# A selective-scan layer: one quarter of B's product on GpSimd, one activation table for exp and ln, and another order for the first chunk

## The chip, the cores and the metric

The kernel runs on one core of a Trainium2 chip. A core has five engines that work in parallel, each with its own queue of instructions in order: TensorE (PE, matrix products into PSUM), VectorE (DVE), ScalarE (ACT, activation functions), GpSimd (POOL) and SyncE (SP, which here issues the transfers). Engines wait for each other through semaphores. The metric is the device time of one execution in microseconds (us), the median of several runs.

## The reference

Four images of 256 channels and 64 x 64 positions pass through four residual layers, each `x = x + layer(groupnorm(x))`. Layers 0 to 2 (a deformable convolution, an attention and a deformable aggregation) are not touched. Layer 3 is a Mamba block over the 4096 positions taken as a sequence:

```
xz = xs @ in_proj_w.T;  u, res = split(xz)            # 512 channels each
u = silu(causal_conv4(u) + conv_b)
dt, Bm, Cm = split(u @ x_proj_w.T)                    # 16, 16, 16
delta = softplus(dt @ dt_proj_w.T + dt_proj_b)
state = exp(delta * A) * state + delta * Bm * u       # 512 x 16 states, per position
y = sum over n of state * Cm  +  u * D
out = (y * silu(res)) @ out_proj_w.T
```

## The kernel before

Images are worked one after the other. For each, layer 3 (`layer3`) cuts the sequence into 8 chunks of 512 positions, and keeps the 512 channels as 4 groups of 128 partitions. A **step** is one state n of one chunk: 8 chunks x 16 states, 128 steps for an image. In a step

- TensorE spreads row n of B over the partitions, as a product of a 0/1 matrix with `bp` into the PSUM tile `bn` (L1419; `bn` has one buffer, so the next row waits until the product has read this one);
- VectorE multiplies `h = du * bn` (L1491, 128 x 2048), du being delta times u;
- ScalarE makes `da = exp(delta * A)` for each group of channels (L1498, two PSUM buffers);
- VectorE runs the recurrence as four scans (L1499);
- GpSimd keeps the last column (`carry`, L1510) and multiplies `h` by row n of C, `cn` (L1513). `cn` is fetched by SP from a small DRAM tensor `cd`, spread over 128 partitions (L1417, six buffers);
- TensorE adds h to `y` through an identity matrix (L1411), two steps behind (`add`).

Beside the steps of chunk j runs the preparation of chunk j+1 (`front`), cut into small parts that are hung into numbered half steps: normalise (`xn`, L1245), project (L1213), convolve (L1259, a product with diagonal matrices), silu (L1273), the product for dt, B and C (L1282, `dbc`), softplus as Abs, Relu, exp and ln (L1303 to L1330), the gates (L1213 again) and a split of B into three bf16 terms (`split`, L1342 to L1350). Seen from the running chunk, these parts begin in step 12 with xn, the convolutions fall in steps 14, 15, 0 and 1, silu in step 2, `dbc` in step 3, and ln in step 9; for the first chunk they come two steps later. The output of chunk j-1 is projected in steps 7 and 9 of chunk j (`close`, L1369). Statistics of the next image (L152) run on VectorE in between.

The order on TensorE, ScalarE, VectorE and GpSimd is the order in which the code emits the instructions (`tc.manual_schedule`). SP's order is left to the planner.

`first()` prepares chunk 0 before any step. It projects and convolves by turns on TensorE, copies on VectorE, applies silu, makes `dbc`, and computes softplus with the differences on VectorE. What of chunk 1's preparation would fall before step 0 (normalising on GpSimd and three projections through one PSUM bank) follows it from the list `begin`. ScalarE has to load a table before a function that the loaded one lacks; the kernel has such loads at silu, at exp and at ln.

Of the kernel before, what the change touches and what calls it, by code (L numbers as in the profile page):

```python
# [9 lines left out]
F32 = mybir.dt.float32  # L10
I32 = mybir.dt.int32
BF16 = mybir.dt.bfloat16
AF = mybir.ActivationFunctionType
# [3 lines left out]
P = 128  # L17
# [46 lines left out]
class Net:  # L64
# [1016 lines left out]
    def layer3(self, x, out, nxt, early):  # L1081
# [4 lines left out]

        nc, tc = self.nc, self.tc
        C = 512
        NC, LEAD = N // C, 4
        with (  # L1090
# [29 lines left out]
            tiny = pa.tile([P, 1], F32, tag="tiny", name="tiny")  # L1120
# [4 lines left out]

            def first():


                c = chunks[0]
                spare = lambda: py.tile([P, C], F32, tag="y", name="front")  # L1130
                xn = pa.tile([P, 2, C], F32, tag="xn3", name="xn3")
# [12 lines left out]
                def project(dc):  # L1144
                    pu = spare()
                    for ct in range(2):
                        nc.tensor.matmul(pu, win[:, ct, bass.ts(dc, P)], xn[:, ct, :], start=(ct == 0), stop=(ct == 1))
                    nc.vector.tensor_copy(up[:, dc, 3:], pu)

                def convolve(dc):  # L1150
                    cv = spare()
                    for i in range(4):
                        nc.tensor.matmul(cv, conv[:, dc, i, :], up[:, dc, i : i + C], start=(i == 0), stop=(i == 3))
                    nc.scalar.activation(u[:, dc, :], cv, AF.Silu, bias=cb[:, dc : dc + 1])

                project(0)
                project(1)
                convolve(0)
                project(2)
                convolve(1)  # L1160
                project(3)
                nc.gpsimd.tensor_copy(tail, up[:, :, C : C + 3])
                convolve(2)
                convolve(3)
                px = bank()
                for dc in range(4):
                    nc.tensor.matmul(px, xpw[:, dc, :], u[:, dc, :], start=(dc == 0), stop=(dc == 3))
                nc.scalar.activation(tiny, self.eps, AF.Exp)
                dbc = pa.tile([P, C], F32, tag="dbc", name="dbc")
                nc.scalar.copy(dbc, px)  # L1170
                c["cd"] = self.dram.tile([DS, C], F32, tag="cd", name="cd")
                nc.sync.dma_start(out=c["cd"], in_=dbc[16:32, :])
# [4 lines left out]

                c["gates"] = [spare() for _ in range(4)]
                for dc, pg in enumerate(c["gates"]):
                    for ct in range(2):  # L1180
                        nc.tensor.matmul(
                            pg, win[:, ct, bass.ts(4 + dc, P)], xn[:, ct, :], start=(ct == 0), stop=(ct == 1)
                        )
# [4 lines left out]
                for lo, hi in ((0, 64), (64, 96), (96, 128)):  # L1188
                    nc.gpsimd.tensor_copy(bp[lo:hi], dbc[lo:hi])
                    if hi < P:  # L1190
                        nc.gpsimd.tensor_copy(t[hi:], dbc[hi:])
                        nc.gpsimd.tensor_sub(dbc[hi:], dbc[hi:], t[hi:])
                for dc in range(4):
                    nc.scalar.activation(w[:, dc, :], pzs[dc], AF.Abs, bias=dtb[:, dc : dc + 1])
                    nc.scalar.activation(du[:, dc, :], w[:, dc, :], AF.Exp, scale=-1.0)
                    nc.vector.tensor_scalar(delta[:, dc, :], pzs[dc], dtb[:, dc : dc + 1], 0.0, ALU.add, ALU.max)
                    nc.vector.tensor_scalar_add(w[:, dc, :], du[:, dc, :], 1.0)
                    nc.vector.scalar_tensor_tensor(
                        du[:, dc, :], w[:, dc, :], -1.0, du[:, dc, :], ALU.add, ALU.subtract
                    )  # L1200
                    nc.vector.tensor_sub(delta[:, dc, :], delta[:, dc, :], du[:, dc, :])
                for dc in range(4):
                    nc.scalar.activation(w[:, dc, :], w[:, dc, :], AF.Ln)
                    nc.vector.tensor_add(delta[:, dc, :], delta[:, dc, :], w[:, dc, :])
                    nc.vector.tensor_mul(du[:, dc, :], delta[:, dc, :], u[:, dc, :])
# [25 lines left out]
            def front(j):  # L1231
# [6 lines left out]
                def begin():  # L1238
                    xn = c["xn"] = pa.tile([P, 2, C], F32, tag="xn3", name="xn3")
                    for ct in range(2):  # L1240
                        to, xs, m, a = xn[:, ct, :], x[:, ct, bass.ts(j, C)], rs[:, ct : ct + 1], shift[:, ct : ct + 1]
                        if j == 1:
                            nc.gpsimd.tensor_scalar(to, xs, m, a, ALU.mult, ALU.add)
                        else:
                            nc.scalar.activation(to, xs, AF.Identity, bias=a, scale=m)  # L1245
                    c["up"] = pa.tile([P, 4, C + 3], F32, tag="up", name="up")
                    nc.gpsimd.tensor_copy(c["up"][:, :, 0:3], tail)
                    c["u"] = pb.tile([P, 4, C], F32, tag="u", name="u")
# [23 lines left out]
                def silu():  # L1272
                    nc.scalar.activation(c["u"], c["u"], AF.Silu)  # L1273
                    gate_silu(j - 1)

# [8 lines left out]
                def keep():  # L1284
                    c["dbc"] = pa.tile([P, C], F32, tag="dbc", name="dbc")
                    nc.scalar.copy(c["dbc"], c["b"])

                    c["cd"] = self.dram.tile([DS, C], F32, tag="cd", name="cd")
                    nc.sync.dma_start(out=c["cd"], in_=c["dbc"][16:32, :])
# [123 lines left out]
            def state(j, n):  # L1413

                c = chunks[j]
                cn = c["cn", n] = pb.tile([P, 1, C], F32, tag="cn", name="cn", bufs=6)
                nc.sync.dma_start(out=cn, in_=c["cd"][n : n + 1, :].unsqueeze(0).to_broadcast([P, 1, C]))  # L1417
                bn = c["bn", n] = pbb.tile([P, 1, C], F32, tag="bn", name="bn")
                nc.tensor.matmul(bn[:, 0, :], pick[:, n, :], c["bp"], start=True, stop=True)  # L1419
# [3 lines left out]
            begin = []  # L1423
            for j in range(1, NC):
                for step, half, pe, rest in front(j):
                    at = DS * (j - 1) - (LEAD if j > 1 else 2) + step
                    if at < 0:
                        begin.append((pe, rest))
                    else:
                        slots.setdefault((at, half), []).append((pe, rest))  # L1430
# [5 lines left out]
            slots.setdefault((last + 2, 0), []).append((None, lambda: gate_silu(NC - 1)))  # L1436
# [33 lines left out]
            with tc.manual_schedule(  # L1470
# [8 lines left out]
                for pe, rest in begin:  # L1479
                    if pe:  # L1480
                        pe()
                    rest()
                state(0, 0)
# [3 lines left out]
                for s in range(total):  # L1487
                    j, n = s // DS, s % DS
                    c = chunks[j]
                    h = pb.tile([P, 4, C], F32, tag="h", name="h", bufs=4)  # L1490
                    nc.vector.tensor_mul(h, c["du"], c.pop(("bn", n)).to_broadcast([P, 4, C]))  # L1491
# [12 lines left out]
                    scan(1)  # L1504
                    empty(s, 0)
# [12 lines left out]
                    if s + 1 < total:  # L1518
                        state((s + 1) // DS, (s + 1) % DS)
# [134 lines left out]
```

## Time and profile before

| what | us |
|---|---|
| median of 3 runs (lowest, highest) | 9984.5 (9975.76, 9988.26) |
| the profiled execution, its own time | 9981.35 |
| its span, first to last instruction | 9979.5 |
| first image: layers 0 to 2 up to layer 3's first norm | 1516.5 |
| first image: preparation, to the first product of step 0 | 55.2 |
| first image: 128 steps | 959 |
| busy of the span: PE, DVE, ACT, POOL | 8624.9, 7632.5, 4959.9, 6758.0 |

The four images repeat the same pattern; their first products of layer 3 (L1491) start at 1571.7, 4045.1, 6517.5 and 8993.3 us. The granted TensorE clock is 0.956 on average.

A row of the timeline reads: start in us, duration in us, engine, line of the kernel, operation, tile written <- tiles read, shapes, count; in brackets, how long the engine was idle before it and which instruction ended that. A row of the page's costliest groups reads: line, engine, operation, tiles, shapes, count | busy us, mean ns of one | idle us before them, and what ended most of it. A matrix product in f32 shows as two passes, each with a MATMUL of its own.

### The profile page before, as it was taken

To read this page: it belongs to the slowest core of one execution; us is meant where nothing else is said; L and a number is where in the kernel's file an instruction comes from. 1 tells how busy PE (TensorE), PEld (TensorE's weight loads), DVE (VectorE), ACT (ScalarE), POOL (GpSimd) and SP (SyncE) were. 2 spreads that over 40 slices of the span, in tenths; PEclk is the share of its full clock that TensorE was granted. 3 is DMA by queue.
4 is the path that set the end of the run, shared out by engine and by line. 5 is a ranking of instruction groups with operands and counts; after the bars stand their busy time and mean duration, and the time that the engine had idled before them with its cause. 6 is when DMAs were issued, how large, how long until landed. Compare 5 with 4: busy or idle time off the path is not lost. (4 is left out here: it accounts for less than half of the span.)

```text
span 9979.5 us, 88756 instructions
## 1 busy us (share of the span) xinstructions
PE 8624.9 (86%) x29193; PEld 4231.9 (42%) x29193; DVE 7632.5 (76%) x8183; ACT 4959.9 (50%) x7576; POOL 6758.0 (68%) x3948
## 2 busy tenths in 40 slices
PE   5889998998778999899877899989977789998997
PEld 3643443333464344333346434433335643443333
DVE  4764597999676459899967646889996764679998
ACT  3743335665474332566557433266645733326664
POOL 3746786887574667688747467768875746777876
PEclk9999999999899999999989999999998999999999
DMA  7830011111793011111188201111118810111111
GB/s 264 319 138 1 31 48 38 46 45 49 258 329 113 1 34 52 36 46 45 44 293 324 82 1 40 48 40 44 45 42 313 322 63 1 42 52 34 40 41 33
DMA packets 377891, 956.56 MB, mean 96 GB/s; under 512 B 34675, under 2 KB 107820, under 8 KB 375372
## 3 DMA queue, kind: packets, MB, share of 16 engines
q0 software_dynamic: 165888, 604.05, 16.8%
q1 hardware_dynamic: 211532, 346.73, 11.1%
q8 instruction: 234, 3.83, 0.2%
q14 instruction: 237, 1.94, 0.1%
HBM read 784.59 MB, written 92.32 MB: 88 GB/s over the span
## 5 line engine op out<-in xcount | busy, mean ns | idle before, releaser
L1499 DVE TENSOR_TENSOR_SCAN h<-da,carry,h 128x512 f32<-128x512 f32 x2048 | 2470.5, 1264 | 138.3 <-ACT da L1498 89.7
L1513 POOL TENSOR_TENSOR h<-h,cn 128x2048 f32<-128x2048 f32 x508 | 2300.1, 4528 | 41.0 <-POOL carry L1510 0.2
L1498 ACT ACTIVATE da<-delta,l3a 128x512 f32<-128x512 f32 x2048 | 1389.1, 689 | 1138.6 <-DVE h L1499 1136.4
L1411 PE MATMUL y<-h,ident 128*128 128x512 f32 x4096 | 1930.8, 616 | 3.3 <-POOL h L1513 2.5
L344 POOL DMA_INDIRECT g<-tab,idx x1152 | 1355.1, 1176 | 756.7 <-issue 368.8
L565 POOL TENSOR_TENSOR acc<-acc,e 128x1024 f32<-128x1024 f32 x480 | 1125.2, 2344 | 541.6 <-ACT e L561 520.1
L388 PE MATMUL pz<-cols,l0w 128*128 128x256 f32 x4608 | 1216.2, 411 | 191.5 <-DVE cols L377 81.3
L1411 PEld LDWEIGHTS y<-h,ident 128*128 128x128 f32 x4096 | 809.8, 198 | 1295.1 <-issue 1233.3
L1491 DVE TENSOR_TENSOR h<-du,bn 128x2048 f32<-128x2048 f32 x512 | 1157.8, 2261 | 34.4 <-PE bn L1419 34.3
L353 DVE SCALAR_TENSOR_TENSOR r<-g,wx,r 128x512 f32<-128x512 f32 x1152 | 858.1, 745 | 368.2 <-ACT r L352 252.2
L462 DVE TENSOR_REDUCE m<-pm 128x3 f32<-128x1536 f32 (+2 forms) x340 | 599.3, 1763 | 699.7 <-PE pm L452 699.7
L388 PEld LDWEIGHTS pz<-cols,l0w 128*128 128x128 f32 x4608 | 896.4, 205 | 361.2 <-DVE cols L377 119.1
L561 ACT ACTIVATE e<-sc 128x1024 f32<-128x1024 f32 x512 | 496.0, 1020 | 1029.7 <-PE sc L548 1029.7
L572 PE MATMUL cx<-e,v 128*128 128x512 f32 x2048 | 1001.1, 616 | 0.0
L845 DVE TENSOR_TENSOR prod<-ring,A 128x1280 f32<-128x1280 f32 x640 | 922.6, 1480 | 79.1 <-DMA ring<-ring 60.8
L352 ACT ACTIVATE r<-g,wx 128x512 f32<-128x512 f32 x1152 | 826.4, 717 | 258.9 <-DMA g<-tab,idx 212.9
L862 PE MATMUL pacc<-prod,ident 128*128 128x512 f32 x1920 | 912.9, 609 | 35.3 <-DVE prod L845 23.3
L854 POOL TENSOR_TENSOR prod<-prod 128x512 f32<-128x512 f32 x640 | 800.1, 1274 | 184.2 <-DVE prod L845 161.6
L370 PE MATMUL pt<-ident,acc 128*128 128x128 f32 x2304 | 426.7, 294 | 297.2 <-DVE acc L361 232.9
L1510 POOL COPY carry<-h 128x4 f32<-128x4 f32 x512 | 98.0, 191 | 804.6 <-DVE h L1499 793.0
L572 PEld LDWEIGHTS cx<-e,v 128*128 128x128 f32 x2048 | 352.4, 189 | 599.1 <-issue 596.6
L360 ACT ACTIVATE acc<-r,wy 128x256 f32<-128x256 f32 x1152 | 571.9, 496 | 24.6 <-DVE r L353 22.1
(254 smaller groups left out, 10959.9 us busy)
## 6 DMA issues: line engine op xcount, KB each, us to landing
cn<-cd SPq DMA_DIRECT2D x512, 256.0 KB
tab<-vt SPq DMA_DIRECT2D x112, 640.0 KB
ring<-ring SPq DMA_DIRECT2D x288, 126.0 KB
ring<-ring SPq DMA_DIRECT2D x288, 124.0 KB
g<-tab,idx POOLq DMA_INDIRECT x1152
x<-in_x SPq DMA_DIRECT2D x64, 256.0 KB
out<-x SPq DMA_DIRECT2D x56, 256.0 KB
l0w<-in_l0w SPq DMA_DIRECT2D x4, 2304.0 KB
```

Source lines behind the costliest of these rows:

```text
L344: nc.gpsimd.indirect_dma_start(out=g[:], out_offset=None, in_=tab[:, :], in_offset=bass.IndirectOffsetOnAxis(ap=idx[:, t, k : k + 1], axis=0),
L353: nc.vector.scalar_tensor_tensor(r, g[:, :, 1, :], wx[:, 1, t, k : k + 1], r, ALU.mult, ALU.add)
L388: nc.tensor.matmul(sums[m][:, ot, :256], wf[:, i, bass.ts(ot, P)], cols[m][:, i, :], start=(i == 0), stop=(i == 17),)
L565: nc.gpsimd.tensor_add(b["acc"], b["acc"], e)
L572: nc.tensor.matmul(blocks[qb]["cx"], v[:, 4 * (i + kt // 4 * 4) + kt % 4, :], e[:, bass.ts(i % 2, 512)], start=(kt == 0 and i == 0), stop= ...
L845: nc.vector.tensor_mul(d["prod"][:, :, t, :].rearrange("p x (g c) -> p x g c", c=GC), ring[y // VR % 4][:, :, y % VR, :].rearrange("p x (g ...
L862: nc.tensor.matmul(d["pd"], self.ident, prod[:, wx, :], start=(wy == 0 and wx == 4), stop=(wy == WIN - 1 and wx == 2),)
L1411: nc.tensor.matmul(c["ys"][dc], self.ident, h[:, dc, :], start=False, stop=(n == DS - 1))
L1491: nc.vector.tensor_mul(h, c["du"], c.pop(("bn", n)).to_broadcast([P, 4, C]))
L1498: nc.scalar.activation(da, c["delta"][:, dc, :], AF.Exp, scale=al[:, dc, n : n + 1])
L1499: nc.vector.tensor_tensor_scan(h[:, dc, :], da, h[:, dc, :], carry[:, dc, n : n + 1], ALU.mult, ALU.add)
L1513: nc.gpsimd.tensor_mul(h, h, cn.to_broadcast([P, 4, C]))
```

## The change

It has four parts, all in `layer3`.

1. In the eight steps n = 14, 15, 0, 1, 2, 3, 4, 5 of each chunk VectorE's product covers three of the four channel groups, and GpSimd multiplies the fourth (`quarter`). GpSimd does not read `bn`: for these steps row n of B comes like `cn` from DRAM. `cd` now holds the rows of C and B, and SP fetches `bs` with two buffers; `cn` has four. Both are issued two steps ahead (`ahead`). `quarter(s + 1)` stands in GpSimd's queue in the middle of step s, ahead of its carry copy and product with cn.
2. After each silu the table set with both exp and ln is loaded by name (`tables`).
3. `first()` is ordered anew. All four projections come first; groups 0 and 2 are copied by ScalarE and convolved on TensorE, groups 1 and 3 are copied and convolved by VectorE (one product and three multiply-adds). In softplus, ScalarE makes Relu and GpSimd the subtraction, the split of B lies between those, and ln of a group follows exp of the next.
4. Chunk 1's normalising moves forward on GpSimd, and its three projections go into three PSUM banks, ahead of chunk 0's gates. The list `begin` is gone.

```diff
-                for dc in range(4):
-                    nc.tensor.matmul(px, xpw[:, dc, :], u[:, dc, :], start=(dc == 0), stop=(dc == 3))
-                nc.scalar.activation(tiny, self.eps, AF.Exp)
+                for dc in range(4):
                     pu = spare()
...
+                    project(pu, xn, dc)
+                    if dc % 2:
+                        nc.vector.tensor_copy(up[:, dc, 3:], pu)
+                        nc.vector.tensor_scalar_mul(u[:, dc, :], up[:, dc, :C], cw[:, dc, 0:1])
+                        for i in range(1, 4):
+                            nc.vector.scalar_tensor_tensor(
+                                u[:, dc, :], up[:, dc, i : i + C], cw[:, dc, i : i + 1], u[:, dc, :], ALU.mult, ALU.add
+                            )
+                    else:
+                        nc.scalar.copy(up[:, dc, 3:], pu)
...
+                    nc.gpsimd.tensor_scalar(
+                        c1["xn"][:, ct, :], x[:, ct, C : 2 * C], rs[:, ct : ct + 1], shift[:, ct : ct + 1], ALU.mult, ALU.add
+                    )
...
+                for dc in (0, 2):
                     cv = spare()
                     for i in range(4):
                         nc.tensor.matmul(cv, conv[:, dc, i, :], up[:, dc, i : i + C], start=(i == 0), stop=(i == 3))
+                    nc.scalar.activation(u[:, dc + 1, :], u[:, dc + 1, :], AF.Silu, bias=cb[:, dc + 1 : dc + 2])
                     nc.scalar.activation(u[:, dc, :], cv, AF.Silu, bias=cb[:, dc : dc + 1])
...
+                for k, dc in enumerate((1, 3, 0, 2)):
+                    nc.tensor.matmul(px, xpw[:, dc, :], u[:, dc, :], start=(k == 0), stop=(k == 3))
+                tables()
...
+                pus = []
+                for dc in range(3):
+                    pus.append(pda.tile([P, C], F32, tag="da", name="front") if dc else bank())
+                    project(pus[dc], c1["xn"], dc)
...
                 for dc in range(4):
                     nc.scalar.activation(w[:, dc, :], pzs[dc], AF.Abs, bias=dtb[:, dc : dc + 1])
                     nc.scalar.activation(du[:, dc, :], w[:, dc, :], AF.Exp, scale=-1.0)
-                    nc.vector.tensor_scalar(delta[:, dc, :], pzs[dc], dtb[:, dc : dc + 1], 0.0, ALU.add, ALU.max)
+                    nc.scalar.activation(delta[:, dc, :], pzs[dc], AF.Relu, bias=dtb[:, dc : dc + 1])
...
-                    nc.vector.tensor_sub(delta[:, dc, :], delta[:, dc, :], du[:, dc, :])
+                    nc.gpsimd.tensor_sub(delta[:, dc, :], delta[:, dc, :], du[:, dc, :])
+                    if dc < 3:
+                        split(*((0, 64), (64, 96), (96, 128))[dc])
+                    if dc:
+                        end(dc - 1)
+                end(3)
+                for dc in range(3):
+                    nc.scalar.copy(c1["up"][:, dc, 3:], pus[dc])
...
                     nc.scalar.activation(c["u"], c["u"], AF.Silu)
                     gate_silu(j - 1)
+                    tables()
...
+            hs, helped = {}, (14, 15, 0, 1, 2, 3, 4, 5)
+
+            def ahead(s):
+
+                if s < NC * DS:
+                    j, n = s // DS, s % DS
+                    c = chunks[j]
+                    for name, r, bufs in (("cn", n, 4), ("bs", DS + n, 2)):
+                        if name == "cn" or n in helped:
+                            t = c[name, n] = pb.tile([P, 1, C], F32, tag=name, name=name, bufs=bufs)
+                            nc.sync.dma_start(
+                                out=t, in_=c["cd"][r : r + 1, :].unsqueeze(0).to_broadcast([P, 1, C])
+                            )
...
+            def quarter(s):
+
+                if s < NC * DS:
+                    c = chunks[s // DS]
+                    hs[s] = pb.tile([P, 4, C], F32, tag="h", name="h", bufs=4)
+                    if s % DS in helped:
+                        nc.gpsimd.tensor_mul(hs[s][:, 3:4, :], c["du"][:, 3:4, :], c.pop(("bs", s % DS)))
...
-                    h = pb.tile([P, 4, C], F32, tag="h", name="h", bufs=4)
-                    nc.vector.tensor_mul(h, c["du"], c.pop(("bn", n)).to_broadcast([P, 4, C]))
+                    h = hs.pop(s)
+                    d = 3 if n in helped else 4
+                    nc.vector.tensor_mul(
+                        h[:, :d, :], c["du"][:, :d, :], c.pop(("bn", n)).to_broadcast([P, d, C])
+                    )
+                    ahead(s + 2)
...
                     scan(0)
                     scan(1)
+                    quarter(s + 1)
                     empty(s, 0)
```

## The prediction

> **What bounds the kernel now.** I began with the page: VectorE is 76% busy over the span, GpSimd 68%, TensorE 86%, so no single engine explains it. The windows by stage then put the change's reach at four stretches of about 1016 us (layer 3 of each image): a preparation of 55.2 us, from 1516.5 to 1571.7 in the first image, in which VectorE is busy for 21 us and TensorE for 47.8, and 128 steps in which VectorE is busy over 96% of the time. The costliest rows of the page are those steps:
>
> ```profile
> L1499 DVE TENSOR_TENSOR_SCAN h<-da,carry,h 128x512 f32<-128x512 f32 x2048 | 2470.5, 1264 | 138.3 <-ACT da L1498 89.7
> L1513 POOL TENSOR_TENSOR h<-h,cn 128x2048 f32<-128x2048 f32 x508 | 2300.1, 4528 | 41.0 <-POOL carry L1510 0.2
> L1491 DVE TENSOR_TENSOR h<-du,bn 128x2048 f32<-128x2048 f32 x512 | 1157.8, 2261 | 34.4 <-PE bn L1419 34.3
> ```
>
> A plain step is 2.26 us of L1491 and four scans, 7.09 us from one L1491 to the next. That says "VectorE". The timeline says which steps that is true of. Here are VectorE's products from step 14 of one chunk to step 3 of the next:
>
> ```profile
> 2158.25 2.26 DVE L1491 TENSOR_TENSOR h<-du,bn 128x2048 f32<-128x2048 f32 x1
> ...
> 2165.81 2.29 DVE L1491 TENSOR_TENSOR h<-du,bn 128x2048 f32<-128x2048 f32 x1 [0.39 <-PE bn L1419]
> ...
> 2172.93 2.26 DVE L1491 TENSOR_TENSOR h<-du,bn 128x2048 f32<-128x2048 f32 x1
> ...
> 2195.72 2.46 DVE L1499 TENSOR_TENSOR_SCAN h<-da,carry,h 128x512 f32<-128x512 f32 x2 [1.60 <-ACT da L1498]
> 2198.09 2.26 DVE L1491 TENSOR_TENSOR h<-du,bn 128x2048 f32<-128x2048 f32 x1
> ```
>
> and TensorE in the same stretch:
>
> ```profile
> 2165.32 0.38 PE L1419 MATMUL bn<-bp,pickn 128*128 128x512 bf16 x1
> 2165.54 3.60 PE L1411 MATMUL y<-h,ident 128*128 128x512 f32 x8
> 2168.97 3.60 PE L1259 MATMUL front<-up,conv 128*128 128x512 f32 x8
> 2172.41 0.38 PE L1419 MATMUL bn<-bp,pickn 128*128 128x512 bf16 x1
> ```
>
> TensorE has no gap: 8 passes for y, 8 for the next chunk's convolution, one for bn, 2172.41 - 2165.32 = 7.09 us. VectorE's product waits for that bn. **Steps 15, 0 and 1 are TensorE's**, and happen to cost what VectorE costs. Step 2 (10.99 us) is ScalarE's: it starts from the last convolution and ends at the exp that the scan waited 1.60 us for:
>
> ```profile
> 2186.78 0.69 ACT L1264 ACTIVATE u<-front,l3b 128x512 f32<-128x512 f32 x1 [1.22 <-PE front L1259]
> ...
> 2188.67 1.28 ACT L1273 ACT_TABLE_LOAD   x1
> 2189.97 1.91 ACT L1273 ACTIVATE u<-u 128x2048 f32<-128x2048 f32 x1
> 2191.78 1.89 ACT L1229 ACTIVATE sres<-sres 128x2048 f32<-128x2048 f32 x1
> 2193.69 1.28 ACT L1498 ACT_TABLE_LOAD   x1
> ```
>
> Before that, TensorE's row at 2145.73 (first projection, fed by xn in step 12) starts a chain without slack to 2165.32. So steps 12 to 2 are a fixed 54.0 us; only steps 3 to 11 are free to follow VectorE.
>
> **Part 1: GpSimd takes a quarter of the product in steps 14, 15, 0 to 5.** Eight products of 16 shrink from 2048 to 1536 elements. Slope between two VectorE rows: (2.259 - 1.225)/1024 = 1.01 ns per element (L1491 and L1515), so 512 elements are 0.52 us; a step becomes 6.57. Counted everywhere that is 256 x 0.52 = 133 us. By the rows above it pays only where VectorE sets the step:
> - Chunks 1 to 5: steps 3, 4, 5: 1.56 us. In 14, 15, 0, 1 it becomes a wait for bn; in 2 a wait for exp.
> - Chunk 6 (no next front in its steps 14 and 15): 5 x 0.52 = 2.6.
> - Chunk 7 (no front at all): 8 x 0.52 = 4.2.
> - Chunk 0: steps 1, 2, 3, 5 give 2.1; step 0 falls from 7.57 to 6.57 (its table load and late copies go), 1.0; step 4 (10.5 us) is the silu chain, nothing.
>
> The cost falls on GpSimd. Its nearest rows are L1513 over four, 1.13 us, and L854 at 1.27; the worst is L1192, 1.65 beside VectorE. I take 1.2. Its period in a helped step is 4.53 + 0.19 + 1.2 + some 0.3 between = 6.2 us, under 6.57, and it lies ahead of the carry copy and h x cn in GpSimd's queue, which TensorE's sum takes up two steps later, so over 5 us of cover. The tight place is step 15, where `du` of the next chunk (L1330, 4.53 us) stands ahead: quarter 15 ends at 2170.0 by the middle-chunk rows, scan 3 wants it at 2171.1; in chunk 0 it is late by 0.3 us, which I charge. The added row fetches (256 of 256 KB) are like L1417's and are issued two steps, some 13 us, ahead on SP's queue, behind cn of the same step; cn's buffers fall from 6 to 4, still two steps of cover. I charge nothing; without that cover, each late row would stall GpSimd's carry and h x cn. Floor 0, ceiling about 1 us per chunk.
>
> The Trainium skill speaks against such a transfer: "SBUF — State Buffer", "Who interferes with whom", says that a VectorE instruction with two SBUF inputs contends with a GpSimd instruction that reads SBUF. The row that shows it is L1516, 3.38 us for half of an h that takes 2.26 by L1513's rate, beside L1515. In the steps VectorE's second operand (bn, da) lies in PSUM and L1513 stays at 4.51 to 4.57, so I use 1.2; with 1.12 more for every quarter GpSimd would reach 7.3 us in a helped step.
>
> **Part 2: one table for exp and ln.** In the loop this removes Ln's load and exp's reload, 2 x 1.28 us per chunk in ScalarE's queue, at step 9 (11 in chunk 0). In the last image, where nothing else hides it:
>
> ```profile
> 9424.10 1.28 ACT L1326 ACT_TABLE_LOAD   x1
> 9425.39 1.91 ACT L1326 ACTIVATE w<-w 128x2048 f32<-128x2048 f32 x1
> 9427.32 1.28 ACT L1498 ACT_TABLE_LOAD   x1
> ```
>
> Without both, the next exp is ready before the scan needs it, so the whole stall goes: 2.05 us in chunk 0, 1.36 in chunks 1 to 6 of the last image, but 0.36 in the others, where two statistics of the next image (L152, 1.0 us) fill VectorE meanwhile. Half of these 0.36 I drop, since TensorE reaches step 12 no earlier where its sums in step 8 ran slowly (5.29 us for 8 passes against 3.60). The skill ("ScalarE: Activation LUTs", "What ACT_TABLE_LOAD costs") gives 2.66 us for a switch, a drain included; here the instruction after the load starts 1.29 us after it began. By the page the pair would be 5.3 us, but the gain would be the same: it is capped by the wait that VectorE has.
>
> Sum of the loop: chunk 0: 2.1 + 1.0 + 2.05 - 0.3 = 4.9; chunks 1 to 5: 5 x (1.56 + 0.2) = 8.8 (last image 5 x 2.92 = 14.6); chunk 6: 2.9 (4.0); chunk 7: 4.2. That is 20.8 for three images, 27.7 for the last: **90 us**.
>
> **Part 3: the first chunk's preparation.** Today it ends with a chain through one PSUM bank: project, copy, project, and then bn:
>
> ```profile
> 1562.60 0.58 ACT L1217 COPY up<-front 128x512 f32<-128x512 f32 x1 [4.92 <-PE front L1213]
> 1567.06 0.59 ACT L1217 COPY up<-front 128x512 f32<-128x512 f32 x1 [3.87 <-PE front L1213]
> 1571.48 0.59 ACT L1217 COPY up<-front 128x512 f32<-128x512 f32 x1 [3.83 <-PE front L1213]
> ```
>
> The new order, from TensorE's start at 1517.2. Four projections: 5.1 us for the first two as now, 8 passes x 0.43 = 3.4 for the others, to 1525.8. Two convolutions on TensorE, 16 passes, 6.9, to 1532.7. VectorE's two (copy 0.69, product 0.42 to 0.73, three accumulations of 0.69 to 0.98 each) end near 1527 and 1531, beside them. The product with xpw: 3.4, of which the last quarter waits for silu (0.69): 1536.2, where it now is 1543.8. dbc copy 0.58, then 1.2 to the first Abs: 1538.1. ScalarE: Abs, exp and now Relu, 0.7 + 0.54 + 0.57 = 1.8 us per part, plus Ln 0.63; VectorE's first difference is out at 1540.9. From there GpSimd's queue is the longest: four subtractions (1.16 to 1.65 each; L1344 and L1192) and the split of dbc, whose seven rows take 6.7 today: 10.1 to 12.3 us, to 1551.0 to 1553.2. Then one add and one product on VectorE, 1.4: 1552.4 to 1554.6, against 1571.7. ScalarE ends by 1549.7, gates by 1548.3, bn follows the split. Chunk 1's normalisation (L1243, 2.50 us) moves to GpSimd's idle stretch before dbc, its three projections (5.2 us of TensorE) to between the dtw products and the gates while ScalarE works, their copies (1.7 us) behind the last Ln; uncovered they would cost these times. The cd write doubles to 64 KB on SP, 10 us and more before its first use by quarter 0. I take 1553.5: 18.2, say **18 us per image, 72 in all**. Were each GpSimd instruction to wait out a VectorE one (the port rule read as a full block), the subtractions are 1.86 each and the start 1 to 2 us later.
>
> **Sum.** 90 + 72 = 162 us. The profiled execution took 9981.35 us, its span 9979.5; the median shown is 9984.5, 3 us above, so I subtract there: **9822 us**.
>
> **Rivals.**
> - *VectorE stays the bound in all steps* (TensorE moves up with it). 133 + 23 of table stalls + 2 + 72 = 230: 9754. For it: VectorE at 96%. Against: the gapless TensorE rows. 12%.
> - *The preparation gains half*: GpSimd's alternating queue and the two waits on it per part stretch to about 1561. 90 + 40: 9854. 16%.
> - *The loads stay* or come back at each change between exp and Ln. In the preparation these alternate: 7 x 1.28 = 9 us per image, and the loop loses its 22: 162 - 36 - 22 = 104: 9880. 6%.
> - *Slower: GpSimd becomes the bound.* Per chunk it has 16 x 5.0 + 4 x 4.53 + 2.5 for the splits = 100.6, plus 8 quarters of 1.2 = 110 of 117.6 us. A quarter of 2.15 us fills it; from 2.8 us, 5.1 more per chunk, the 162 are used up. At 3.2, each with the 1.12 of L1516 and a late row, about 126 per chunk: 32 x 8.4 = 270 lost against the forecast: 10090. For it: GpSimd runs 2 us behind at step 13 already. Against: bn and da in PSUM. 6%.
>
> The forecast itself 58%; 2% for no change. A measurement of this kernel can tell about 0.2%, 20 us. Faster 0.92, same 0.02, slower 0.06. The range takes in the second rival, most of the way to the first, and the unknown costs: 9764 to 9868.
>
> **What would show it.** L1491's successor: 256 products of 128x1536 near 1.74 us; GpSimd quarters near 1.2. Steps 3, 4, 5 at 6.57; steps 15, 0, 1 still at 7.09, with more idle on VectorE released by bn; step 2 still near 11. No load at Ln. First product about 36 us after the first projection instead of 54.5. It is wrong if steps 14 to 1 shorten, if scans wait for GpSimd, or if TensorE's rows in steps 12 to 15 close up.

## The result

| | before | after |
|---|---|---|
| median of 4 runs (lowest, highest), us | 9980.13 (9975.66, 9988.26) | 9836.97 (9825.3, 9840.41) |
| the profiled execution, us | 9981.35 | 9825.3 |
| its span, us | 9979.5 | 9823.5 |
| granted TensorE clock, mean | 0.956 | 0.959 |

The ratio is 0.9855, with an interval of 0.9841 to 0.9869: 143 us faster by the medians. The forecast was 9822.

The two traces, cut at the same instructions, say where it came from. "128 steps" runs from the first product of step 0 to the product of the last step; "preparation" from the last L176 of the norm (its line in both kernels) to that first product. Each figure is a sum over four images.

| stretch, us | before | after | gain | forecast |
|---|---|---|---|---|
| 128 steps | 3803.0 | 3711.7 | 91.3 | 90 |
| preparation | 214.0 | 164.2 | 49.8 | 72 |
| the rest: layers 0 to 2, both ends | 5962.5 | 5947.6 | 14.9 | 0 |

The last row is not the change's: its code is the same in both, and the profiled execution of after was the fastest of its four. The change is worth 141 us by these two traces, with the steps where the forecast had them and the preparation 22 us short.

The costliest rows of after that answer to those of before (the page's groups):

```profile
L1548 DVE TENSOR_TENSOR_SCAN h<-da,carry,h 128x512 f32<-128x512 f32 x2048 | 2469.0, 1264 | 138.3 <-ACT da L1547 78.0
L1563 POOL TENSOR_TENSOR h<-h,cn 128x2048 f32<-128x2048 f32 x508 | 2299.7, 4527 | 41.3 <-POOL carry L1560 0.8
...
L1537 DVE TENSOR_TENSOR h<-du,bn 128x2048 f32<-128x2048 f32 (+1 forms) x512 | 1022.8, 1998 | 49.9 <-PE bn L1460 49.8
```

Scans and GpSimd's products with cn cost what they did. B's product lost 1157.8 - 1022.8 = 135 us of VectorE's work, the 133 of the prediction's first reckoning. Only half of that came out of the time, and the row says why: its idle time, all of it released by bn, grew from 34.4 to 49.9 us. VectorE's products from step 14 of one chunk to step 3 of the next (the timeline of VectorE, after):

```profile
2137.02 1.73 DVE L1537 TENSOR_TENSOR h<-du,bn 128x1536 f32<-128x1536 f32 x1
...
2144.51 1.75 DVE L1537 TENSOR_TENSOR h<-du,bn 128x1536 f32<-128x1536 f32 x1 [0.86 <-PE bn L1460]
...
2151.59 1.75 DVE L1537 TENSOR_TENSOR h<-du,bn 128x1536 f32<-128x1536 f32 x1 [0.42 <-PE bn L1460]
...
2158.68 1.75 DVE L1537 TENSOR_TENSOR h<-du,bn 128x1536 f32<-128x1536 f32 x1 [0.42 <-PE bn L1460]
...
2165.76 1.75 DVE L1537 TENSOR_TENSOR h<-du,bn 128x1536 f32<-128x1536 f32 x1 [0.42 <-PE bn L1460]
...
2174.48 2.46 DVE L1548 TENSOR_TENSOR_SCAN h<-da,carry,h 128x512 f32<-128x512 f32 x2 [2.21 <-ACT da L1547]
2176.86 1.73 DVE L1537 TENSOR_TENSOR h<-du,bn 128x1536 f32<-128x1536 f32 x1
```

The rows are steps 14, 15, 0, 1, 2, then the scan that ends step 2, then step 3. From 15 to 2 the starts stay 7.08 us apart, and before each product VectorE now stands idle, 0.86 us and then three times 0.42, for bn. Step 2 is 11.10 us (10.98 before): the scan's wait for exp grew from 1.60 to 2.21 us and swallowed the shorter product. Step 3 is 6.56. TensorE beside them (timeline, after) has the rows that it had, 2151.18 - 2144.09 = 7.09 us from one bn to the next and no idle between:

```profile
2144.09 0.38 PE L1460 MATMUL bn<-bp,pickn 128*128 128x512 bf16 x1
2144.31 3.60 PE L1438 MATMUL y<-h,ident 128*128 128x512 f32 x8
2147.74 3.60 PE L1285 MATMUL front<-up,conv 128*128 128x512 f32 x8
2151.18 0.38 PE L1460 MATMUL bn<-bp,pickn 128*128 128x512 bf16 x1
```

And ScalarE at ln in chunk 0 (timeline, after), where before had a table load ahead of L1326's ln and one behind it:

```profile
1644.44 1.30 ACT L1547 ACTIVATE da<-delta,l3a 128x512 f32<-128x512 f32 x2
1645.77 1.91 ACT L1353 ACTIVATE w<-w 128x2048 f32<-128x2048 f32 x1
1647.85 0.69 ACT L1547 ACTIVATE da<-delta,l3a 128x512 f32<-128x512 f32 x1 [0.17 <-DVE h L1548]
```

exp, ln and exp follow one another without a load, and the exp behind ln waits for a scan, no longer the scan for it: step 11 of chunk 0 went from 9.21 to 7.09 us. In the whole kernel the loads fell from 168 to 104.

### The profile page after: what moved, and what is told of

Its sections match the earlier page's. It is cut to its first block, busy times and chain, and to the rows that moved or that the text cites. A ratio compares the mean times of both kernels' runs of the same rounds, so it can differ in the third digit from the quotient of the medians.

```text
span 9823.5 us, 89566 instructions
## 1 busy us (share of the span) xinstructions
PE 8552.6 (87%) x29129; PEld 4208.7 (43%) x29129; DVE 7522.1 (77%) x8175; ACT 4893.9 (50%) x7532; POOL 7112.0 (72%) x4220
## 5 line engine op out<-in xcount | busy, mean ns | idle before, releaser
L1563 POOL TENSOR_TENSOR h<-h,cn 128x2048 f32<-128x2048 f32 x508 | 2299.7, 4527 | 41.3 <-POOL carry L1560 0.8
L1438 PE MATMUL y<-h,ident 128*128 128x512 f32 x4096 | 1907.6, 610 | 12.4 <-POOL h L1563 12.4
L1537 DVE TENSOR_TENSOR h<-du,bn 128x2048 f32<-128x2048 f32 (+1 forms) x512 | 1022.8, 1998 | 49.9 <-PE bn L1460 49.8
L361 DVE SCALAR_TENSOR_TENSOR acc<-r,wy,acc 128x256 f32<-128x256 f32 x1152 | 548.6, 477 | 0.0
```

Source lines behind the costliest of these rows:

```text
L1438: nc.tensor.matmul(c["ys"][dc], self.ident, h[:, dc, :], start=False, stop=(n == DS - 1))
L1537: nc.vector.tensor_mul(h[:, :d, :], c["du"][:, :d, :], c.pop(("bn", n)).to_broadcast([P, d, C]))
L1563: nc.gpsimd.tensor_mul(h, h, cn.to_broadcast([P, 4, C]))
```

## The experiments

All of them change after, but for experiment 5, which changes before, and 8, which changes nothing. They ran on three chips: 1 to 4 on the first, 5 to 7 on the second, 8 to 10 on the third; 1 to 5 have one execution each. On the first and the third chip layers 0 to 2, which no edit touches, took 5763 to 5786 us with the ends, on the second and in the two traces above 5948 to 5968. So totals are compared on one chip only, and the stretches of layer 3 between chips. Where a kernel ran again unchanged (after, in experiment 8) its 128 steps summed to 3717.2 instead of 3711.7: about 5 us is what such a sum can tell.

**1. The quarter in steps 3, 4 and 5 alone.** The theory is the prediction's: in 14 to 2 of the middle chunks it is worth nothing.

```diff
-            hs, helped = {}, (14, 15, 0, 1, 2, 3, 4, 5)
+            hs, helped = {}, (3, 4, 5)
```

> The changed kernel with GpSimd's quarter in steps 3, 4 and 5 alone. Measure: the four stretches from the first product of step 0 to the last step's product, 3803.0 us before and 3711.7 after in sum. Theory (TensorE sets steps 14, 15, 0, 1 of chunks with a next front, ScalarE step 2): only steps 0 to 2 of chunk 0, 14 and 15 of chunk 6 and 0 to 2, 14 of chunk 7 lose 0.53 us each, about 5 us per image: 3732. Rival (VectorE sets all steps, each quarter pays 0.53): five of eight quarters gone, 85 us lost: 3796.

The 128 steps took 3728.1 us (9682.52 in all, before on that chip 9786.4). Five quarters in eight were taken away and 16.4 us of 91.3 went with them, most of that due in chunks 6 and 7, which have no convolution beside steps 14 and 15 or none at all. The theory's 3732 holds, 3796 does not.

**2. No quarter at all.** This leaves the table and the new preparation.

```diff
-            hs, helped = {}, (14, 15, 0, 1, 2, 3, 4, 5)
+            hs, helped = {}, ()
```

> The changed kernel without any quarter: VectorE multiplies all four groups in every step. Theory: the quarters are worth about 17 us per image in the loop, so 3712 + 67 = 3779. Rival (each of 256 pays 0.53): 3712 + 136 = 3848, slower than the loop before.

3782.7 us (9736.92 in all). The quarters are worth 3782.7 - 3711.7 = 71 us, of which the three of experiment 1 make 55.

**3. Two tables again.** The load by name goes, and exp and ln each load their own.

```diff
                     gate_silu(j - 1)
-                    tables()
...
-            slots.setdefault((last + 2, 0), []).append((None, lambda: (gate_silu(NC - 1), tables())))
+            slots.setdefault((last + 2, 0), []).append((None, lambda: gate_silu(NC - 1)))
```

> The changed kernel without the load by name in the loop, so that ln and the exp behind it load their tables again (first chunk's preparation unchanged). Theory: only the wait that VectorE had comes back: 2.1 to 3.9 us in chunk 0, 0.2 to 0.4 in chunks 1 to 6 of three images, 1.4 in those of the last: 22 to 29 us, loop 3734 to 3741. Rival (each load costs its 1.28 us): 2 x 1.28 x 7 x 4 = 72, loop 3784.

3739.2 us (9672.28 in all), with 160 loads: 27.5 us for the table. Each of parts 1 and 2 taken away from after costs 71 and 27.5, together 98.5, more than the 91.3 that both bring; taken alone they bring 3803.0 - 3739.2 = 63.8 and 3803.0 - 3782.7 = 20.3. That one part helps the other is not shown by this: in the middle chunks the table is worth the same with and without the quarters (step 9 falls from 8.44 to 8.08 us in both), and 5.2 of the 7.2 us of difference lie in chunks 0 and 1, where single steps change from one execution to the next (experiment 9).

**4 and 5. One tap of the convolution, in after and in before.** If TensorE's convolution is what holds steps 15, 0 and 1 at 7.09, then taking three quarters of it away must shorten them in after, where VectorE needs 6.56, and not in before, where VectorE needs 7.09 as well. These two leave out three of four taps in chunks 1 to 7 and compute nothing else differently.

```diff
-                        for i in range(4):
+                        for i in (3,):
                             nc.tensor.matmul(
-                                c["b"], conv[:, dc, i, :], c["up"][:, dc, i : i + C], start=(i == 0), stop=(i == 3)
+                                c["b"], conv[:, dc, i, :], c["up"][:, dc, i : i + C], start=True, stop=True
```

In after:

> The changed kernel with one tap instead of four in the convolutions on TensorE for chunks 1 to 7 (leaves out three quarters of these convolutions), which takes 2.6 us from TensorE in steps 14, 15, 0 and 1. Theory (TensorE hides the quarters there): these steps fall from 7.5 to 8.3 and 7.08 to 6.56, step 2 from 11.1 to about 10.2, since silu no longer waits for the last convolution; 3.4 us per middle chunk, loop about 3637. Rival (these steps wait for GpSimd or something else): they stay at 7.08, loop 3712.

In before:

> The kernel before with one tap instead of four in the same convolutions (leaves out three quarters of these convolutions). Theory: VectorE is as slow as TensorE in steps 15, 0 and 1, so these stay at 7.09; step 14 falls from 7.56 to 7.09, step 2 from 10.98 to about 10.1: 1.3 us per middle chunk, loop about 3773. Rival (TensorE alone was the bound there): steps 15, 0, 1 fall below 7.0.

After with one tap took 3643.7 us, before with one tap 3770.4. VectorE's products of steps 14, 15 and 0 (timeline of VectorE, after with one tap):

```profile
2073.72 1.73 DVE L1537 TENSOR_TENSOR h<-du,bn 128x1536 f32<-128x1536 f32 x1
...
2080.28 1.73 DVE L1537 TENSOR_TENSOR h<-du,bn 128x1536 f32<-128x1536 f32 x1
...
2086.83 1.73 DVE L1537 TENSOR_TENSOR h<-du,bn 128x1536 f32<-128x1536 f32 x1
```

6.56 us apart, and none waits for bn. TensorE now waits for VectorE (its timeline, same kernel):

```profile
2086.32 1.02 PE L1285 MATMUL front<-up,conv 128*128 128x512 f32 x2
2088.61 0.38 PE L1460 MATMUL bn<-bp,pickn 128*128 128x512 bf16 x1 [1.28 <-DVE h L1537]
```

In before with one tap the steps stay where they were (timelines of VectorE and of TensorE):

```profile
2163.02 2.26 DVE L1491 TENSOR_TENSOR h<-du,bn 128x2048 f32<-128x2048 f32 x1
...
2170.11 2.26 DVE L1491 TENSOR_TENSOR h<-du,bn 128x2048 f32<-128x2048 f32 x1
```

```profile
2172.43 0.38 PE L1419 MATMUL bn<-bp,pickn 128*128 128x512 bf16 x1 [2.07 <-DVE h L1491]
```

7.09 us, with TensorE idle for 2.07 of them. So with one tap the change brings 3770.4 - 3643.7 = 126.7 us in the steps, against 91.3 with all four: TensorE's convolution keeps 35 us of it. For steps 15, 0 and 1 that is the rival "VectorE sets all steps" made true by hand. Step 2 fell to 10.24 us in both kernels, near the 10.2 and 10.1 expected; what is left of it is the chain through silu and exp on ScalarE, and there the change brings nothing.

**6. The subtraction of softplus back on VectorE, in the new preparation.** The trace of after showed the preparation ending 3.4 us later than worked out, with long rows on VectorE and GpSimd by turns (timelines of after, VectorE and GpSimd):

```profile
1551.19 1.53 DVE L1217 TENSOR_TENSOR du<-delta,u 128x512 f32<-128x512 f32 x1
1552.64 1.48 DVE L1223 TENSOR_SCALAR w<-du 128x512 f32<-128x512 f32 x1
...
1563.06 0.69 DVE L1217 TENSOR_TENSOR du<-delta,u 128x512 f32<-128x512 f32 x1
1563.67 1.75 DVE L1537 TENSOR_TENSOR h<-du,bn 128x1536 f32<-128x1536 f32 x1
```

```profile
1550.70 1.48 POOL L1212 TENSOR_TENSOR dbc<-dbc,bt 64x512 f32<-64x512 f32 x1
1552.25 1.59 POOL L1227 TENSOR_TENSOR delta<-delta,du 128x512 f32<-128x512 f32 x1
...
1557.26 1.59 POOL L1227 TENSOR_TENSOR delta<-delta,du 128x512 f32<-128x512 f32 x1
...
1560.32 1.55 POOL L1227 TENSOR_TENSOR delta<-delta,du 128x512 f32<-128x512 f32 x1 [0.71 <-DVE du L1224]
```

The same product takes VectorE 1.53 us beside GpSimd's subtraction and 0.69 when that is done, at 1563.06. All of these instructions read SBUF alone.

```diff
-                    nc.gpsimd.tensor_sub(delta[:, dc, :], delta[:, dc, :], du[:, dc, :])
+                    nc.vector.tensor_sub(delta[:, dc, :], delta[:, dc, :], du[:, dc, :])
```

> The changed kernel with softplus's subtraction in the first chunk back on VectorE. Measure: from the reciprocal of the last norm (L176) to the first product of step 0, 55.6 us before and 40.9 after. Theory (GpSimd and VectorE block each other there): VectorE gets four times 0.69 us, but loses the waits for four GpSimd instructions of 1.27 to 1.59 us and most of the stretching of its rows from 0.42 to 1.48 and 0.69 to 1.53 us; about 38 us, 12 us less for four images. Rival (VectorE's own work is the bound): 2.8 us longer, 43.7.

The mean of the four preparations fell from 41.05 to 39.6 us, so it is better, and by about half of what the theory said. Part of the difference is scatter: up to GpSimd's copy `up<-tail` (L1193) the preparations of one kernel differ by some 1 us, in after by 1.2. From that copy to the first product they took 23.9 us in all four images of after and 22.0 in all four here, 1.9 less. The time is 9830.46 us (9822.64 to 9839.54), its ratio to before 0.9855 (0.9839 to 0.9872): not to be told from after. GpSimd's last instruction of the split (its timeline, this kernel):

```profile
1549.53 0.95 POOL L1209 CAST bp<-dbc 32x512 bf16<-32x512 f32 x1
```

ends at 1550.48, and VectorE's rows on either side of that moment (its timeline, this kernel):

```profile
1543.17 0.43 DVE L1223 TENSOR_SCALAR w<-du 128x512 f32<-128x512 f32 x1 [8.75 <-ACT du L1221]
...
1545.03 1.39 DVE L1223 TENSOR_SCALAR w<-du 128x512 f32<-128x512 f32 x1
...
1548.37 1.64 DVE L1216 TENSOR_TENSOR delta<-delta,w 128x512 f32<-128x512 f32 x1
...
1550.95 0.41 DVE L1223 TENSOR_SCALAR w<-du 128x512 f32<-128x512 f32 x1
...
1552.81 0.69 DVE L1216 TENSOR_TENSOR delta<-delta,w 128x512 f32<-128x512 f32 x1
```

go from 1.39 to 0.41 and from 1.64 to 0.69. These are VectorE instructions of one kind and one size, with GpSimd at work and with GpSimd done. ScalarE, too, is busy before that moment and mostly idle behind it, but the row at 1543.17 takes 0.43 us with ScalarE at work and GpSimd idle (from 1541.91 to 1544.48): the stretching goes with GpSimd. That GpSimd is stretched in turn is in after's subtractions, 1.27 us for the first, which begins while VectorE is idle, and 1.55 to 1.59 for the other three. The split alone still stretches five rows of VectorE, by 2.7 us together; that this is what kept the gain below the theory's is likely, but no run takes the split away.

**7. And the addition of 1 on ScalarE.** This takes four of VectorE's rows out of the stretch as well.

```diff
-                    nc.vector.tensor_scalar_add(w[:, dc, :], du[:, dc, :], 1.0)
+                    nc.scalar.activation(w[:, dc, :], du[:, dc, :], AF.Identity, bias=self.ones[:, 0:1])
...
-                    nc.gpsimd.tensor_sub(delta[:, dc, :], delta[:, dc, :], du[:, dc, :])
+                    nc.vector.tensor_sub(delta[:, dc, :], delta[:, dc, :], du[:, dc, :])
```

> As the run with the subtraction on VectorE, and the sum 1 + exp of the first chunk made by ScalarE. Theory: ScalarE, idle for some 6 us in that stretch, takes 4 x 0.57 us, VectorE loses four rows that were up to 1.48 us beside GpSimd: about 36 us, 20 us less than the changed kernel for four images. Rival (ScalarE's chain Abs, exp, Relu, ln becomes the longest): no better than the run without it, about 38.

38.6 us on average (21.1 to 21.2 from GpSimd's copy on), 9824.2 in all (9817.31 to 9833.15), ratio 0.985 (0.9834 to 0.9867): one microsecond better than experiment 6, where two were expected. What is next in line is TensorE (its timeline, this kernel):

```profile
1539.91 12.18 PE L1152 MATMUL front<-xn,l3a 128*128 128x512 f32 x28
1551.92 0.38 PE L1460 MATMUL bn<-bp,pickn 128*128 128x512 bf16 x1
```

28 passes for chunk 1's three projections and chunk 0's gates, then bn, with the first product at 1553.52. The moved projections are 12 of the 28, 5.2 us. TensorE ends 1.2 us before the first product, so a saving of more than that in softplus would, by estimate, leave these projections on the path.

**8. After once more, unchanged,** on the chip of the two versions that follow.

> The changed kernel once more, beside the next two on one chip. Loop near 3712, preparation near 164 for four images, 143 us under the kernel before.

9643.8 us (9633.88 to 9664.07) against before's 9775.9 on that chip, ratio 0.9855 (0.9836 to 0.9874), the same as in the first comparison. Its steps took 3717.2, its preparations 166.2.

**9. The quarter in all 16 steps of chunk 7,** on top of experiment 7. Chunk 7 has no next chunk to prepare, so no convolution holds TensorE.

```diff
-            hs, helped = {}, (14, 15, 0, 1, 2, 3, 4, 5)
+            hs = {}
+
+            def helps(s):
+                return s % DS in (14, 15, 0, 1, 2, 3, 4, 5) or s // DS == NC - 1
...
-                        if name == "cn" or n in helped:
+                        if name == "cn" or helps(s):
...
-                    if s % DS in helped:
+                    if helps(s):
...
-                    d = 3 if n in helped else 4
+                    d = 3 if helps(s) else 4
```

> The run with subtraction on VectorE and sum on ScalarE, and in chunk 7, which has no next chunk's preparation beside it, a quarter in every step. Theory (steps 6 to 13 of chunk 7 are VectorE's, GpSimd has 6.3 us of work in a step): eight steps fall from 7.09 to 6.56, 17 us for four images, loop about 3695; with the shorter preparation 27 us less than the changed kernel. Rival (two row fetches in each step come late): chunk 7 no shorter, 3712.

Chunk 7 gave what was expected, 429.3 to 411.9, 17.4 us over the four images. But the 128 steps took 3706.3 where 3695 was expected: chunk 1 took 467.6 in sum against 462.5 and chunk 0 483.7 against 482.9, for instance 9.04 us in step 13 of chunk 0 that is otherwise 7.09. Three of the four images have such a step here, the last image of experiment 8 has one, and after has none. With it chunks 0 and 1 take 239.0 to 239.3 us of an image, without it 233.9 to 235.6 in these three kernels. The trace of experiment 8 shows where it comes from (timeline of TensorE, first image and last):

```profile
1594.28 5.13 PE L1438 MATMUL y<-h,ident 128*128 128x512 f32 x8
1601.01 1.98 PE L1242 MATMUL front<-xn,l3a 128*128 128x512 f32 x4 [1.60 <-ACT xn L1271]
...
8783.49 3.59 PE L1438 MATMUL y<-h,ident 128*128 128x512 f32 x8
8790.38 3.78 PE L1242 MATMUL front<-xn,l3a 128*128 128x512 f32 x4 [3.29 <-ACT xn L1271]
```

In the first image TensorE is slow in the sum for y, where nothing waits for it; in the last it is slow in the projection of step 12 (granted clock 0.62 over 9 us there, 1.00 over the same stretch of the first image). ScalarE's copies and then an exp come late by it, and VectorE's scan in step 13 waits 1.82 us for that exp. What places the slow stretch is open. The time is 9622.52 (9611.79 to 9637.2), ratio 0.9835 (0.9818 to 0.9851).

**10. And steps 6 and 7 of every chunk.**

```diff
-                return s % DS in (14, 15, 0, 1, 2, 3, 4, 5) or s // DS == NC - 1
+                return s % DS in (14, 15, 0, 1, 2, 3, 4, 5) or s // DS == NC - 1 or s % DS in (6, 7)
```

> As the run with chunk 7 in full, and quarters in steps 6 and 7 of every chunk too. Theory (these steps are VectorE's): they fall to 6.56, but step 8 waits 0.5 us more for GpSimd's addition of step 6 (L1319's successor), so 0.5 to 1 us per chunk: loop 3668 to 3682. Rival (GpSimd has no room: 113 of 117 us): du of the next chunk comes late at step 0, loop 3695 or more.

The steps took 3679.7 us, within the theory's 3668 to 3682. Of the 26.6 us against experiment 9, 12.9 lie in chunks 0 and 1, where the long steps of that run are shorter here; chunks 2 to 6 gave 13.8, or 0.7 per chunk and image, as the theory had it. Steps 6 and 7 are 6.56; step 8 gives half of one back, 7.90 against 7.38, since it waits for exp behind ScalarE's addition in softplus, which waits for GpSimd (timelines of ScalarE and of VectorE):

```profile
2035.41 2.00 ACT L1351 ACTIVATE du<-w,ones 128x2048 f32<-128x2048 f32 x1 [2.10 <-POOL delta L1346]
```

```profile
2038.03 2.46 DVE L1551 TENSOR_TENSOR_SCAN h<-da,carry,h 128x512 f32<-128x512 f32 x2 [0.70 <-ACT da L1550]
```

9610.92 us (9579.2 to 9614.45), ratio 0.9817 (0.9797 to 0.9836). This is the fastest version tried: 33 us, 0.34%, below after on the same chip, and the two kernels' runs do not overlap.

## Why the prediction was right, and where it was not

**What bounds the steps: right.** The reading that TensorE, not VectorE, sets steps 15, 0 and 1, and ScalarE step 2, decided the size of part 1. It forecast nothing for five of the eight shortened products in the middle chunks, and experiments 1, 4 and 5 show that. Its 54.0 us from step 12 to the end of step 2 stayed: 54.0 in the middle chunks of before, 54.0 to 54.8 in after. By chunk, in us summed over four images:

| chunk | before | after | gain | forecast |
|---|---|---|---|---|
| 0 | 493.6 | 479.2 | 14.4 | 19.6 |
| 1 | 478.1 | 460.8 | 17.3 | 8.2 |
| 2 to 5, each | 477.9 | 469.8 | 8.1 | 8.2 |
| 6 | 475.8 | 463.2 | 12.6 | 12.7 |
| 7 | 443.8 | 429.2 | 14.6 | 16.8 |

The total of 90 is right to 1.3 us. Chunks 0 and 1 have to be read together, 31.7 against 27.8, since a stall in the one comes back in the other (below). Within them misses cancel, and that is luck. Steps 3 and 4 of chunk 0 went from 7.09 to 7.03 and from 10.51 to 11.10 us, where the prediction had a gain of 0.52 and nothing: TensorE works there without a gap from 1575.91 on, so step 3 is TensorE's as well. Against that, steps 13 and 14 fell from 7.91 to 7.09 and from 9.16 to 8.22, which no step of the prediction had; the passes of the projection in step 12 took up to 1.22 us each in before and 0.70 at most in after, so step 13 at least goes with TensorE's rate, as in experiment 9. Chunk 7 stayed 2 us short because the stretch ends at the product of its last step: seven helped steps lie in it, 7 x 0.53 x 4 = 14.8, and not eight.

**GpSimd's quarter: right.** It measured 1.27 us in the median against the estimate of 1.2, lowest 1.25, highest 1.30; the product of three groups 1.73 to 1.75 against 1.74. L1563 beside it stayed at 4.53. The rule of the Trainium skill that spoke against the transfer ("SBUF — State Buffer", "Who interferes with whom") did not bite here, where VectorE's second operand lies in PSUM. The slower rival, which needed quarters of 2.8 us, is excluded.

**The late quarter: the size wrong, the net right by luck.** "In chunk 0 quarter 15 is late by 0.3 us, which I charge." The wait itself is nine times that (timelines of GpSimd and of VectorE in step 15 of chunk 0, after):

```profile
1675.98 4.52 POOL L1357 TENSOR_TENSOR du<-delta,u 128x2048 f32<-128x2048 f32 x1
1680.44 1.28 POOL L1468 TENSOR_TENSOR h<-du,bs 128x512 f32<-128x512 f32 x1
```

```profile
1681.76 1.28 DVE L1548 TENSOR_TENSOR_SCAN h<-da,carry,h 128x512 f32<-128x512 f32 x1 [2.61 <-POOL h L1468]
```

GpSimd's du stands ahead of the quarter, as feared, and the scan waits 2.61 us for it. So one of the prediction's signs of being wrong, scans that wait for GpSimd, came true here, once in each image and nowhere else (10.4 us in all). Most of it came back, because the three steps that follow then took 6.56, 6.55 and 10.25 us instead of the 7.08, 7.08 and 11.10 of the middle chunks: from step 15 to step 3 after took 32.66 us against 32.34 with the usual steps, 0.3 more. Part of chunk 1's gain in the table is this return.

**The table: right, and a little more.** The prediction's 22 us for the loop measured 27.5 with the quarters in place and 20.3 without. At the loads themselves step 11 of chunk 0 gained 2.12 us and step 9 of chunks 1 to 6 0.36, 1.36 in the last image: 23 us. The rest of the 27.5 lies mostly in steps 13 to 2 between chunks 0 and 1. The gain is the stall of VectorE, as argued, and not the 1.28 us of each of the 56 loads, which would be 72.

**The preparation: the mechanism right, the term mis-sized, 72 against 49.8.** Two things in it failed.

First, the length of the old preparation was taken for all four images from the first alone. The windows of the four preparations of before (columns: window, us, busy of PE, PEld, DVE, ACT and POOL with counts, granted clock, DMA share, GB/s) would have shown it:

```profile
1516.06:1571.69 55.63, 47.80 (x93) 18.34 (x93) 21.38 (x32) 16.11 (x24) 18.52 (x26) 0.87 0.09 29
3993.75:4045.13 51.38, 43.74 (x93) 17.37 (x93) 21.39 (x32) 16.11 (x24) 18.52 (x26) 0.96 0.10 32
6461.80:6517.50 55.70, 47.87 (x93) 18.40 (x93) 21.42 (x33) 16.25 (x24) 18.55 (x26) 0.87 0.09 29
8941.90:8993.30 51.40, 44.13 (x93) 17.52 (x93) 21.39 (x32) 16.11 (x24) 18.55 (x26) 0.95 0.10 32
```

The same 93 matmuls take TensorE 4 us less in the second and fourth image, at a granted clock of 0.96 and 0.95 instead of 0.87, while VectorE and ScalarE take the same. Two images so took 4.25 us less than the other two, and 2 x 4.25 = 8.5 us were not there to be gained. The difference sits in the chain through one PSUM bank that the prediction quoted as the end of the old preparation; here are its last two projections in the first image and in the second (timeline of TensorE, before):

```profile
1563.24 3.78 PE L1213 MATMUL front<-xn,l3a 128*128 128x512 f32 x4 [0.68 <-ACT up L1217]
1567.69 3.75 PE L1213 MATMUL front<-xn,l3a 128*128 128x512 f32 x4 [0.68 <-ACT up L1217]
...
4040.24 1.98 PE L1213 MATMUL front<-xn,l3a 128*128 128x512 f32 x4 [0.68 <-ACT up L1217]
4042.90 1.98 PE L1213 MATMUL front<-xn,l3a 128*128 128x512 f32 x4 [0.68 <-ACT up L1217]
```

The ScalarE waits of 3.87 and 3.83 us shown there were projections at half rate, which two images of four don't have.

Second, "GpSimd's queue is the longest: 10.1 to 12.3 us" took 14.3, from 1547.58 to 1561.87. Up to there each step fell where it was put: with after's times moved back by the 6.72 us by which its layer 3 began later, convolutions done at 1532.7 (1532.7 forecast), the product with xpw at 1536.3 (1536.2), the first Abs at 1538.2 (1538.1), the first difference at 1540.7 (1540.9). The queue itself was mis-summed: the rows that the prediction names for it, four subtractions of 1.16 to 1.65 us and a split of 6.7, make 11.3 to 13.3. In after the subtractions took 6.0 us and the split 7.1, together 13.1, near the upper end of that. Of the other 1.2 us 0.7 are the wait for VectorE before the last subtraction (shown in experiment 6), and the rest are gaps of 0.04 to 0.08 us between rows. Behind the last subtraction the forecast's 1.4 us took 1.8, because VectorE was still in a product that took 1.64. So VectorE's rows, which the prediction left at 0.42 and 0.69 us and which took up to 1.5 and 1.6, cost some 1.1 us directly, and GpSimd's own queue the larger part.

The rule of the Trainium skill named above ("SBUF — State Buffer", "Who interferes with whom") counts both sides: a VectorE instruction with two SBUF inputs, or one in a two-port mode, which an addition of a constant can enter, shares a port pair with GpSimd, and whoever issues first blocks the other. The rows here agree in that both engines grow, and the prediction applied it to GpSimd's side alone. The end came at 1557.0 instead of 1553.5, 3.5 us in each of four images, 14 in all. Experiments 6 and 7 win back 2.4 of the 3.5 us; since they take rows out of the queue and contention away at once, they do not tell the two apart. No run takes part 3 or part 4 back alone, so the 49.8 us stay undivided between them. The rival "the preparation gains half" put the end at about 1561, as far from the measured one as the forecast, but its gain of 40 us is nearer to 49.8 than the forecast's 72.

**The sum.** The two terms missed make 22 us, and the steps gave 1.3 more. The untouched layers happened to run 14.9 faster in the profiled execution, the median lies 12 us above that execution, and 3 had been added for the median. So the 9822 against 9836.97 is by luck some 6 us nearer than the terms were: of the 162 us forecast, 141 are in these two traces and 134 in experiment 8 (3803.0 + 214.0 - 3717.2 - 166.2).

## What to carry to other kernels

Before counting a saving on the busiest engine, read step by step which engine releases the next step: here 135 us less work on VectorE was worth 71, and taking work off TensorE showed 35 us of the missing part at once. Two engines that hand each other tiles in SBUF by turns must both be costed with each other's load, and a queue of many short rows is to be added up row by row, gaps included. A stretch that repeats is to be measured in each of its repetitions before its gain is multiplied.

## What was not expected of the hardware

- VectorE's short rows with all operands in SBUF grow by up to three and a half times beside GpSimd: a 128x512 f32 add of a constant from 0.41 to 1.39 and 1.48 us, a 128x512 f32 product from 0.69 to 1.53, a sum from 0.69 to 1.64. GpSimd's own 128x512 subtraction grew from 1.27 to 1.59 at the same time, so both sides paid.
- The granted clock can differ over the same instructions in one execution. In the last 14 us of the old preparation it was 0.63 in the first image and 1.00 in the second (windows of before, 1558 to 1572 and 4032 to 4046), with idle times of TensorE of the same 0.68 us between the same products. In before with one tap it was the second and the third image that took longer (55.7 us against 51.4 and 51.6), so it does not go with the image. The Trainium skill ("TensorE: Matmul & The Clock Gate", "Part 1: The HAM clock gate") has the rate halve after an idle window of about 3.4 us, and the windows run on freely of the program. That fits the half rate and its coming and going; but TensorE's longest idle time from 1545 to 1571 is 1.35 us, shorter than such a window, and no run here shows where a window lay, so what halves the rate stays open. In after, where those projections stand between other products, the four preparations are 40.7 to 41.9 us, without two kinds.
